# Linear attention with transposed outputs and divisors, and its jobs spread over steps of eight and six

## The chip, the core and the metric

The kernel runs on one NeuronCore of a Trainium2 chip, in one launch. The metric is the device time of that launch in microseconds (us). Five engines run beside each other, each through its own list of instructions in order: TensorE (PE in the profile; its weight loads have a row of their own, PEld), VectorE (DVE), ScalarE (ACT), GpSimd (POOL) and SyncE (SP, which issues most DMAs). They wait for each other through semaphores. Results of TensorE lie in PSUM, which the other engines read.

## The reference

Four transformer layers run one after the other on `x` (8 batches, 256 tokens, 256 features) with a context of the same shape, all in float32. The second layer, L1, is the one that changes. It has three linear attentions (one in an encoder layer on twice the context, two in a decoder layer on `x`) and two feed-forward blocks (256 to 512 to 256, ReLU), each followed by a layer norm that is added to the residual:

```python
def linear_attention(q, k, v):          # 8 heads of 32
    Q = jax.nn.elu(q) + 1.0
    K = jax.nn.elu(k) + 1.0
    vlen = v.shape[1]
    v = v / vlen
    KV = jnp.einsum('nshd,nshv->nhdv', K, v)
    Z = 1.0 / (jnp.einsum('nlhd,nhd->nlh', Q, K.sum(axis=1)) + EPS_ATTN)
    out = jnp.einsum('nlhd,nhdv,nlh->nlhv', Q, KV, Z) * vlen
    return out
```

The other layers: L0 and L3 have two softmax attentions and a feed-forward block each, L2 two softmax attentions and a mixture of eight experts with two chosen per token.

## The kernel before

All work is cut by batch, 8 units of 256 tokens. `Stream` (L736) holds the order of the work, written out by hand: every unit (`Item` for softmax attention, `Linear`, `Ffn`) puts its jobs at numbered steps, counted from the step at which the unit starts; `Stream.run` walks through the steps and emits the jobs of each, in the order in which they were put. A step has no length of its own: it lasts as long as its work. In an attention stage a step also holds one block of scores. The first stream holds L0, L1 and the attentions of L2; the experts and L3 follow.

L1 is the stretch of steps 160 to about 276. `e1` is the encoder's linear attention, `d0` and `d1` those of the decoder, `e2` and `d2` the feed-forward blocks. `e1`, `d0` and `e2` start a unit every 7 steps, so one of each lies in a period of 7. `d1` and `d2` start one every 4 steps; `d2` follows `d1` 14 steps behind. Before them `f0`, the feed-forward of L0, is still running; after them `sa2`, the self-attention of L2, starts with its projections beside the last `d2`.

The jobs of one `Linear` unit, with their step (L609):

- `turn` (0): TensorE transposes the input through PSUM, ACT copies it out (for `d1` the encoder's output too).
- `queries` (1): 4 matmuls into `ps_lq` (L524); `elu` (L506): DVE takes the minimum with 0 (L509), ACT the exponential (L510), and later DVE joins max(x, 0) with it (L514).
- `keys_values` (2): the joining for the queries, then 8 matmuls into one score tile, `s_kv` (L537), keys and values; the `elu` of the keys; ACT copies the values (`lv`, L544) beside a column of ones.
- `end_keys` (3): the joining for the keys; POOL adds a bias row to x.
- `sums` (4): keys times values (L555) into `ps_kv`; DVE masks the result to blocks of heads (L561) and builds four columns of key sums (L562), together `kv`, 132 wide.
- `mix` (6, twice): queries times `kv` (L569) for 128 tokens each; DVE adds the epsilon to the four divisors of a token, takes reciprocals of 8 numbers per partition (L574) and multiplies (L577).
- `turn_back` (8): TensorE transposes the result (L191), ACT copies it to `oT` (L584).
- `out` (9): 4 matmuls (L591), copied by ACT to `y` (L595). `norm_stats` (10), `norm` (11), `add` (13): the layer norm on DVE and POOL.

`Ffn` (L709) has `turn`, then `hidden` (L652, two of them in L1) and two outputs (L675) in the steps that follow, then its sum, norm and add.

PSUM pools: `ps_m` (2 buffers) for transposes, projections, `ps_kv`, hidden values and outputs; `ps_o` (2 buffers) for `lo` and for `ps_f`, the feed-forward's output; the two score tiles `sq` and `sk`, one each, which a unit of `Linear` uses by the parity of its batch. `y`, 4 buffers, holds the exponentials and the values under a norm.

A matmul of float32 is two records in the profile; an output of 256 columns by 256 inputs (4 matmuls) is "x8".

Of the kernel before, what the change touches and what calls it, by code (L numbers as in the profile page):

```python
# [90 lines left out]
def decoder_stack(ctx: ExitStack, tc: tile.TileContext, t: dict, out: bass.AP):  # L91
# [33 lines left out]
    def con(name):  # L125
        a, b = CONSTS[name]
        return cons[:, a:b]
# [6 lines left out]
    nc.gpsimd.memset(neg_half, -0.5)  # L134
    ones = const.tile([128, 128], F32, name="ones")
# [359 lines left out]
    class Linear:  # L495
# [10 lines left out]
        def elu(self, ps, name, bufs):  # L506

            e = work.tile([128, 2, 256], F32, tag="y", bufs=4, name="elu")
            nc.vector.tensor_scalar(e, ps, 0.0, None, ALU.min)  # L509
            nc.scalar.activation(e, e, AF.Exp)  # L510
            dst = stage_tile(name, bufs=bufs, name="l" + name)

            def rest():
                nc.vector.scalar_tensor_tensor(dst, ps, 0.0, e, ALU.max, ALU.add)  # L514
                return dst

            return rest

        def queries(self):
            w = self.sub["w"]  # L520
            ps = ps_m.tile([128, 2, 256], F32, tag="m", name="ps_lq")
            for i in range(2):
                for c in range(2):
                    nc.tensor.matmul(  # L524
                        ps[:, i, :], lhsT=w[:, c, i * 128 : (i + 1) * 128], rhs=self.xT[:, c, :], start=c == 0, stop=c == 1
                    )
            self.rest_q = self.elu(ps, "q0", 3)

        def keys_values(self):

            self.q = self.rest_q()
            w = self.sub["w"]
            s = scores["pool"].tile([128, 2, 2, 256], F32, tag="sq" if self.b % 2 else "sk", bufs=1, name="s_kv")
            for half in range(2):
                for n in range(2):
                    for c in range(2):
                        nc.tensor.matmul(  # L537
                            s[:, half, n, :], lhsT=self.kvT[:, c, n * 128 : (n + 1) * 128],
                            rhs=w[:, c, 256 + 256 * half : 512 + 256 * half], start=c == 0, stop=c == 1,
                        )  # L540
            self.rest_k = self.elu(s[:, 0], "q1", 3)
            self.v = stage_tile("k", (128, 2, 2, 129), 3, name="lv")
            nc.gpsimd.memset(self.v[:, :, :, 128:129], 1.0)
            nc.scalar.copy(self.v[:, :, :, 0:128], s[:, 1].rearrange("p n (i d) -> p n i d", i=2))  # L544

        def end_keys(self):
            self.k = self.rest_k()

            nc.gpsimd.tensor_tensor(self.x, self.x, over(self.sub["rows"][:, 1, :]), ALU.add)

        def sums(self):
            ps = ps_m.tile([128, 2, 256], F32, tag="m", name="ps_kv")
            for i in range(2):
# [6 lines left out]
            self.kv = kv = stage_tile("oq", (128, 2, 132), name="kv")  # L560
            nc.vector.tensor_tensor(kv[:, :, 0:128], ps[:, :, 0:128], over(con("blocks")), ALU.mult)  # L561
            nc.vector.tensor_tensor(  # L562
                kv[:, :, 128:132], ps[:, :, 128:129].to_broadcast([128, 2, 4]), over(con("heads")), ALU.mult
            )

        def mix(self, n):
            o = ps_o.tile([128, 2, 132], F32, tag="o", name="lo")
            for i in range(2):
                nc.tensor.matmul(  # L569
                    o[:, i, :], lhsT=self.q[:, i, n * 128 : (n + 1) * 128], rhs=self.kv[:, i, :], start=True, stop=True  # L570
                )
            z = small.tile([128, 2, 4, 1], F32, tag="z", name="z")
            nc.vector.tensor_scalar(z[:, :, :, 0], o[:, :, 128:132], 1e-6, None, ALU.add)
            nc.vector.reciprocal(z, z)  # L574
            if n == 0:
                self.o = stage_tile("yo", (128, 2, 256), name="lo_sb")
            nc.vector.tensor_tensor(  # L577
                self.o[:, n, :].rearrange("p (i h d) -> p i h d", i=2, d=32),
                o[:, :, 0:128].rearrange("p i (h d) -> p i h d", d=32), z.to_broadcast([128, 2, 4, 32]), ALU.mult,
            )  # L580

        def turn_back(self):
            self.oT = stage_tile("oT")
            transposed(self.o, lambda ps: nc.scalar.copy(self.oT, ps))  # L584
# [24 lines left out]
        def jobs(self, put):  # L609
            if self.sub.get("begin"):  # L610
                put(-3, self.sub["begin"], self.b)
            put(0, self.turn)
            put(1, self.queries)
            put(2, self.keys_values)
            put(3, self.end_keys)
            put(4, self.sums)
            put(6, self.mix, 0)
            put(6, self.mix, 1)
            put(8, self.turn_back)
            put(9, self.out)  # L620
            put(10, self.norm_stats)
            put(11, self.norm)
            put(13, self.add)

    class Ffn:
# [83 lines left out]
        def jobs(self, put):  # L709
# [3 lines left out]
            put(0, self.turn)  # L713
            n = self.f // 256
            for k in range(n):
                put(1 + k, self.hidden, k)
            if n == 4:
                for k in range(4):
                    put(n + 1 + k, self.out, k // 2, k % 2)
                end = n + 5  # L720
            else:
                for k in range(2):
                    put(n + 1 + k, self.out, k, 0)
                    put(n + 1 + k, self.out, k, 1)
                end = n + 3
# [10 lines left out]
    class Stream:  # L736
# [6 lines left out]
        def put(self, step, f, *args):  # L743
            self.at.setdefault(step, []).append(lambda: f(*args))

        def add(self, unit, start):
            unit.jobs(lambda step, f, *args: self.put(start + step, f, *args))
# [5 lines left out]
        def run(self):  # L753
            before = None
            for step in range(min(self.at), max([*self.at, *self.k]) + 2):
# [7 lines left out]
                for f in self.at.get(step, []):  # L763
                    f()
# [379 lines left out]
    def ffn(f, x, bias, hidden_bias=None, gain=None, post=False, last=False, end=None):  # L1144
        return {
            "f": f, "x": x, "bias": bias, "hidden_bias": hidden_bias, "gain": gain, "post": post, "last": last, "end": end,
        }
# [23 lines left out]
    f0 = ffn(DFF, own_x, 0, "L0_ffn", post=True)  # L1171
    e1 = {"x": the_enc, "kv": None, "begin": enc_first}
    e2 = ffn(2 * D, the_enc, 1, end=enc_store)
    d0 = {"x": own_x, "kv": None}
    d1 = {"x": own_x, "kv": the_enc, "begin": enc_load}
    d2 = ffn(2 * D, own_x, 1)
# [24 lines left out]
    follow(first, Linear, e1, 160, 7)  # L1201
    first.put(141, fill, d0, load_attn, "L1_d0", "L1_d0")
    follow(first, Linear, d0, 164, 7)
    follow(first, Ffn, e2, 174, 7)
    first.put(177, fill, d2, load_ffn, "L1_d", "L1_d2", 2 * D)
    first.put(220, fill, d1, load_attn, "L1_d1", "L1_d1")
    follow(first, Linear, d1, 225, 4)
    first.put(224, fill, sa2, load_attn, "L2_sa")
    follow(first, Ffn, d2, 239, 4)
    start = 239 + 11 + 14  # L1210
    attend(first, sa2, start)
    first.put(264, fill, ca2, load_attn, "L2_ca")
# [5 lines left out]
    f3 = ffn(DFF, own_x, 0, "L3_ffn", gain="L3_3", last=True)  # L1218
# [146 lines left out]
```

## Time and profile before

| | |
|---|---|
| time, median of 3 runs | 2501.59 us (2499.62 to 2510.47) |
| profiled execution | 2498.09 us, span 2496.3 us |
| mean granted TensorE clock | 0.955 |
| busy: PE / PEld / DVE / ACT / POOL | 2205.7 / 1654.2 / 1141.9 / 925.8 / 721.9 us |
| first `queries` of `e1` | 620.34 us |
| first `turn` of `d1` | 925.23 us |
| last `mix` of `d1` ends | about 1081.8 us |
| first step with both kinds of scores in `sa2` | 1129.42 us |

Times inside the span are counted from its start. The L1 stretch is the 509 us between the second and the last of these marks, a fifth of the span. A line of the timeline gives start and length in us, the engine, the line of the kernel, the operation, output and inputs, the count, and in brackets the idle time before it with what ended it. A line of the groups gives count, then busy us and mean ns of one, then idle time before them.

### The profile page before, as it was taken

The page shows a single profiled execution, that of the slowest core. Times are in us where ns is not written, and L with a number is a line of the kernel's source. Part 1 is how long each engine was busy: PE and PEld are TensorE (multiplying, and loading weights), DVE is VectorE, ACT ScalarE, POOL GpSimd, SP SyncE. Part 2 cuts the span into 40 slices and gives each one's busy share as a digit, 9 for nine tenths or more (in the row PEclk, how much of TensorE's full clock was granted, in tenths as well). Part 3 has the DMA queues.
Part 4 walks back from the last instruction along what each step waited for, and adds up shares of the span by engine and source line. Part 5 has one row for each costly group of instructions (what it writes and reads, how often), then busy time and mean ns, then how long its engine had stood idle before and what let it go on. Part 6 is the DMA issues. An engine that isn't in the chain of part 4 may idle for free.

```text
span 2496.3 us, 40268 instructions
## 1 busy us (share of the span) xinstructions
PE 2205.7 (88%) x17118; PEld 1654.2 (66%) x17118; DVE 1141.9 (46%) x2266; ACT 925.8 (37%) x1570; POOL 721.9 (29%) x781
## 2 busy tenths in 40 slices
PE   5888999999887788899999974799999599999899
PEld 4555666578776677776666543588888367766588
DVE  3545566733445454456777652100000355566521
ACT  1333355521222222235666531233332154555421
POOL 1011233333323231442334434222220533122131
PEclk8989999999999999999999987799999699999999
DMA  4170001000000020000000001355554100000000
GB/s 148 59 242 6 1 23 42 2 22 1 22 5 9 5 68 26 1 22 2 1 2 22 16 20 55 132 180 186 182 180 143 46 19 10 1 2 1 1 13 21
DMA packets 57059, 121.05 MB, mean 48 GB/s; under 512 B 6752, under 2 KB 40432, under 8 KB 50992
## 3 DMA queue, kind: packets, MB, share of 16 engines
q0 software_dynamic: 11904, 62.76, 7.1%
q1 hardware_dynamic: 44976, 55.73, 6.8%
q8 instruction: 134, 2.20, 0.4%
q14 instruction: 45, 0.37, 0.1%
HBM read 87.20 MB, written 31.20 MB: 47 GB/s over the span
## 4 chain that ended last, share of the span: by engine, by line
PE 79%; DVE 12%; POOL 2%; ACT 2%; issue 2%; DMA 2%; another core or an unknown queue 0%; SPq 0%; ACTq 0%; POOLq 0%; DVEq 0%
PE s_q L780 15%; PE ps_p L276 7%; PE s_e L1061 7%; PE ps_f L675 7%; PE ps_e L1070 6%; PE ps_h L652 6%; PE o L402 4%; DVE mx L372 4%; PE ps_v L329 4%; PE ps_out L426 4%; PE s_kv L537 3%; PE ps_t L191 3%; PE s_k L780 2%; PE s_q L776 2%; PE s_k L776 2%
## 5 line engine op out<-in xcount | busy, mean ns | idle before, releaser
L372 DVE TENSOR_REDUCE mx<-s_q 128x4 f32<-128x1024 f32 x320 | 392.3, 1226 | 355.9 <-PE s_k L780 310.1
L387 ACT ACTIVATE p<-s_k 128x1024 f32<-128x1024 f32 x320 | 327.8, 1024 | 411.9 <-PE s_k L780 401.0
L780 PE MATMUL s_q<-k,q 32*128 32x256 f32 (+1 forms) x3072 | 433.4, 400 | 28.5 <-DVE mx L372 28.4
L780 PE MATMUL s_k<-q,k 32*128 32x256 f32 (+1 forms) x3072 | 430.4, 398 | 8.8 <-ACT p L387 8.4
L780 PEld LDWEIGHTS s_q<-k,q 32*128 32x128 f32 x3072 | 258.2, 188 | 134.6 <-issue 53.7
L780 PEld LDWEIGHTS s_k<-q,k 32*128 32x128 f32 x3072 | 266.4, 187 | 19.9 <-ACT p L387 14.4
L204 POOL TENSOR_TENSOR rs<-ve,neg_half 128x2 f32<-128x2 f32 x120 | 87.0, 725 | 618.8 <-DVE ve L202 591.0
L414 POOL TENSOR_TENSOR yo<-oq,rec 128x256 f32<-128x256 f32 x96 | 60.0, 625 | 560.0 <-DVE rec L413 557.1
L402 PE MATMUL o<-p,va 128*32 128x256 f32 (+1 forms) x3072 | 201.7, 380 | 1.2 <-ACT p L387 1.2
L1061 PE MATMUL s_e<-eT,fc 128*128 128x256 f32 x736 | 170.7, 388 | 3.7 <-ACT eT L217 3.3
L1075 DVE COPY ye<-ps_e 128x512 f32<-128x512 f32 x23 | 15.9, 691 | 321.5 <-PE ps_e L1070 321.5
L1070 PE MATMUL ps_e<-fc,h 128*128 128x256 f32 x736 | 162.6, 379 | 0.0
L1061 PEld LDWEIGHTS s_e<-eT,fc 128*128 128x128 f32 x736 | 133.7, 192 | 34.4 <-ACT eT L217 6.8
L1070 PEld LDWEIGHTS ps_e<-fc,h 128*128 128x128 f32 x736 | 139.8, 190 | 19.0
L402 PEld LDWEIGHTS o<-p,va 128*32 128x32 f32 x3072 | 80.8, 110 | 94.4 <-issue 57.1
L1065 ACT ACTIVATE h<-s_e,fc 128x256 f32<-128x256 f32 x184 | 87.1, 474 | 143.4 <-PE s_e L1061 134.9
L652 PE MATMUL ps_h<-xT,w_L_w 128*128 128x256 f32 x512 | 121.8, 381 | 0.0
L776 PEld LDWEIGHTS <-ident_b 128*128 128x128 bf16 x1024 | 86.3, 102 | 53.0 <-issue 18.1
L675 PE MATMUL ps_f<-w_L_w,h 128*128 128x256 f32 x512 | 120.5, 379 | 0.0
L652 PEld LDWEIGHTS ps_h<-xT,w_L_w 128*128 128x128 f32 x512 | 96.6, 190 | 15.8 <-issue 2.3
L276 PE MATMUL ps_p<-qT,w_L_sa 128*128 128x256 f32 x384 | 102.5, 414 | 3.1 <-ACT qT L217 1.4
L311 ACT ACTIVATE k<-ps_p,cols,cons 128x256 f32<-128x256 f32 x192 | 97.6, 563 | 20.6 <-PE ps_p L276 14.6
(251 smaller groups left out, 3710.9 us busy)
## 6 DMA issues: line engine op xcount, KB each, us to landing
moe_rows<-zero SPq DMA_DIRECT2D x8, 2048.0 KB, 15.9
moe_results<-ye SPq DMA_DIRECT2D x23, 256.0 KB, 2.3
w_L_w<-in_L_w SPq DMA_DIRECT2D x4, 1024.0 KB
w_L_sa<-in_L_sa SPq DMA_DIRECT2D x3, 1024.0 KB, 5.0
w_L_ca<-in_L_ca SPq DMA_DIRECT2D x3, 1024.0 KB, 5.1
x_nat<-in_x SPq DMA_DIRECT2D x4, 512.0 KB, 6.7
mi<-in_mask_qk SPq DMA_DIRECT2D x8, 256.0 KB, 3.5
c_nat<-in_ctx SPq DMA_DIRECT2D x4, 512.0 KB, 9.8
```

The lines of the kernel that those rows point to most:

```text
L276: nc.tensor.matmul(ps, lhsT=self.w[:, c, at : at + 128], rhs=src[:, c, :], start=c == 0, stop=c == 1)
L329: nc.tensor.matmul(ps, lhsT=self.kv_in[:, c, n * 128 : (n + 1) * 128], rhs=self.w[:, c, 512:768], start=c == 0, stop=c == 1)
L372: nc.vector.tensor_reduce(out, s, AX.X, ALU.max, negate=True)
L387: nc.scalar.activation(p, s, AF.Exp, scale=DH**-0.5)
L402: nc.tensor.matmul(self.o[32 * j : 32 * j + 32, a, q0:], lhsT=self.va[:, kt, 8 * a + 2 * j + par, :], rhs=p[j // 2][:, j % 2, kt, q0:], st ...
L426: nc.tensor.matmul(self.po[:, n, :], lhsT=self.oT[:, a, n * 128 : (n + 1) * 128], rhs=self.w[:, a, 768:1024], start=a == 0, stop=a == 1,)
L652: nc.tensor.matmul(ps[:, i, :], lhsT=w1[:, c, at : at + 128], rhs=self.xT[:, c, :], start=c == 0, stop=c == 1)
L675: nc.tensor.matmul(self.po[:, n, :], lhsT=self.h[f // 4][:, f % 4, n * 128 : (n + 1) * 128], rhs=w2[:, f, :], start=f == 0, stop=f == nf - 1,)
L776: nc.tensor.matmul(o, lhsT=ident_b, rhs=m, start=half == 0, stop=False, skip_group_check=True)
L780: nc.tensor.matmul(o, lhsT=lhsT, rhs=rhs, start=half == 0 and not pen, stop=True, skip_group_check=True)
L1061: nc.tensor.matmul(s[:, i, :], lhsT=w1[:, c * DFF + f * 128 : c * DFF + f * 128 + 128], rhs=hT[:, c, :], start=c == 0, stop=c == 1,)
L1070: nc.tensor.matmul(po[:, n, :], lhsT=hs[f // 4][:, f % 4, n * 128 : n * 128 + 128], rhs=w2[:, f, :], start=f == 0, stop=f == 7,)
```

## The change

`Linear` computes its output already transposed: the second matrix is built with the key sums repeated over each head's block (`kv[:, 1]`, 128 wide) and the matrices become the stationary operands, so one `mix` gives, for all 256 tokens, the divisors (part 1) and the numerators (part 0) with features on partitions. `oT` is their quotient, which `out` takes as it is; `turn_back` is gone. The reciprocal is taken of the full tile, 512 numbers per partition. In `elu` the minimum is now a ReLU of -x on ACT. `queries` write to `ps_o`, `mix` to a score tile; each of `e1`, `d0`, `d1` has score tiles of its own.

`keys_values` is split into `keys` (step 2) and `values` (step 3), `out` comes at 6 instead of 9, and the jobs have ranks: within a step, rank 0 is emitted first, then 1 (the default), 2 and 3. `e1`, `d0` and `e2` now start a unit every 8 steps, `d1` and `d2` every 6; `d2` follows `d1` 11 steps behind and `sa2` starts at step 274 instead of 264. The steps of a feed-forward's jobs are given by hand. The loads of `d1` and `sa2` move by a few steps.

```diff
-        def elu(self, ps, name, bufs):
+        def elu(self, ps, name):
             e = work.tile([128, 2, 256], F32, tag="y", bufs=4, name="elu")
-            nc.vector.tensor_scalar(e, ps, 0.0, None, ALU.min)
-            nc.scalar.activation(e, e, AF.Exp)
+            nc.scalar.activation(e, ps, AF.Relu, scale=-1.0)
+            nc.scalar.activation(e, e, AF.Exp, scale=-1.0)
...
         def queries(self):
-            ps = ps_m.tile([128, 2, 256], F32, tag="m", name="ps_lq")
+            ps = ps_o.tile([128, 2, 256], F32, tag="o", name="ps_lq")
...
+        def end_queries(self):
             self.q = self.rest_q()
-            s = scores["pool"].tile([128, 2, 2, 256], F32, tag="sq" if self.b % 2 else "sk", bufs=1, name="s_kv")
...
+        def home(self, part):
+            return scores["pool"].tile([128, 2, 2, 256], F32, tag=self.sub["homes"][part], bufs=1, name="s_kv")
+        def keys(self):
+            self.s = self.home(0)
+            self.project(0)
+            self.rest_k = self.elu(self.s[:, 0], "q1")
+        def values(self):
+            self.project(1)
             self.v = stage_tile("k", (128, 2, 2, 129), 3, name="lv")
...
-            self.kv = kv = stage_tile("oq", (128, 2, 132), name="kv")
-            nc.vector.tensor_tensor(kv[:, :, 0:128], ps[:, :, 0:128], over(con("blocks")), ALU.mult)
-            nc.vector.tensor_tensor(
-                kv[:, :, 128:132], ps[:, :, 128:129].to_broadcast([128, 2, 4]), over(con("heads")), ALU.mult
-            )
+            self.kv = kv = stage_tile("oq", (128, 2, 2, 128), name="kv")
+            nc.vector.tensor_tensor(kv[:, 0], ps[:, :, 0:128], over(con("blocks")), ALU.mult)
+            nc.vector.tensor_tensor(kv[:, 1], ps[:, :, 128:129].to_broadcast([128, 2, 128]), over(con("blocks")), ALU.mult)
...
-        def mix(self, n):
...
-        def turn_back(self):
-            self.oT = stage_tile("oT")
-            transposed(self.o, lambda ps: nc.scalar.copy(self.oT, ps))
+        def mix(self):
+            self.s = self.home(1)
+            for part in (1, 0):
+                for i in range(2):
+                    nc.tensor.matmul(
+                        self.s[:, part, i, :], lhsT=self.kv[:, part, i, :], rhs=self.q[:, i, :], start=True, stop=True
+                    )
+            z = stage_tile("yo", name="z")
+            nc.scalar.activation(z, self.s[:, 1], AF.Identity, bias=eps_z)
             nc.vector.reciprocal(z, z)
+            self.oT = stage_tile("oT")
+            nc.vector.tensor_tensor(self.oT, self.s[:, 0], z, ALU.mult)
...
-            put(0, self.turn)
-            put(1, self.queries)
-            put(2, self.keys_values)
-            put(3, self.end_keys)
-            put(4, self.sums)
-            put(6, self.mix, 0)
-            put(6, self.mix, 1)
-            put(8, self.turn_back)
-            put(9, self.out)
-            put(10, self.norm_stats)
-            put(11, self.norm)
-            put(13, self.add)
+            put(0, self.turn, rank=2)
+            put(1, self.queries, rank=2)
+            put(2, self.end_queries, rank=0)
+            put(2, self.keys, rank=0)
+            put(3, self.values, rank=0)
+            put(4, self.sums, rank=0)
+            put(5, self.mix, rank=0)
+            put(6, self.out, rank=3)
+            put(7, self.norm_stats, rank=3)
+            put(8, self.norm, rank=3)
+            put(10, self.add)
...
-                for f in self.at.get(step, []):
+                for _, f in sorted(self.at.get(step, []), key=lambda job: job[0]):
                     f()
...
+    e1 = {"x": the_enc, "kv": None, "begin": enc_first, "homes": ("sq", "sq")}
+    d0 = {"x": own_x, "kv": None, "homes": ("sk", "sk")}
+    e2 = ffn(2 * D, the_enc, 1, (1, 2, 5, 6), end=enc_store)
+    d1 = {"x": own_x, "kv": the_enc, "begin": enc_load, "homes": ("sq", "sk")}
+    d2 = ffn(2 * D, own_x, 1, (2, 3, 4, 5))
...
-    follow(first, Linear, e1, 160, 7)
+    follow(first, Linear, e1, 160, 8)
-    follow(first, Linear, d0, 164, 7)
-    follow(first, Ffn, e2, 174, 7)
+    follow(first, Linear, d0, 164, 8)
+    follow(first, Ffn, e2, 174, 8)
-    follow(first, Linear, d1, 225, 4)
+    follow(first, Linear, d1, 225, 6)
-    follow(first, Ffn, d2, 239, 4)
-    start = 239 + 11 + 14
+    follow(first, Ffn, d2, 236, 6)
+    start = 274
     attend(first, sa2, start)
```

## The prediction

> **What bounds the kernel now.** I read the busy shares by stretch first, then TensorE's timeline, the waits on it, and the groups of DVE and ACT. The L1 stretch runs from the first `queries` of `e1` (620.34 us) to the first step with both kinds of scores (1129.42): 509.1 us. The stretches below are `e1`/`d0`/`e2`, `d1`/`d2`, and the way into `sa2`; the columns are length, then busy us of PE, PEld, DVE, ACT, POOL with counts, then the granted clock.
>
> ```profile
> 620.00:925.00 305.00, 246.16 (x1247) 211.58 (x1245) 153.01 (x409) 67.21 (x122) 92.20 (x101) 0.97 0.06 19
> 925.00:1082.00 157.00, 133.28 (x682) 113.91 (x683) 73.61 (x200) 44.79 (x80) 49.22 (x52) 0.97 0.06 17
> 1082.00:1129.00 47.00, 45.98 (x241) 35.63 (x240) 26.42 (x60) 13.96 (x28) 22.92 (x20) 1.00 0.09 29
> ```
>
> TensorE has most of the work in every stretch, but stands idle for 59 and 24 us in the first two. Where, the timeline of one period of 37.6 us shows (from one slow `ps_f` to the next):
>
> ```profile
> 732.31 3.54 PE L675 MATMUL ps_f<-w_L_e_w,h 128*128 128x256 f32 x8 [2.09 <-DVE z L573]
> ...
> 737.12 1.89 PE L675 MATMUL ps_f<-w_L_e_w,h 128*128 128x256 f32 x8
> 738.85 0.60 PE L191 MATMUL ps_t<-cons,lo_sb 128*128 128x128 f32 x4
> 739.29 1.89 PE L524 MATMUL ps_lq<-xT,w_L_d 128*128 128x256 f32 x8
> 741.02 0.61 PE L569 MATMUL lo<-kv,lq 128*128 128x132 f32 x4
> 743.16 0.72 PE L569 MATMUL lo<-kv,lq 128*128 128x132 f32 x4 [1.53 <-ACT y L690]
> ...
> 751.53 0.66 PE L191 MATMUL ps_t<-cons,lo_sb 128*128 128x128 f32 x4 [1.59 <-ACT xT L228]
> ...
> 756.99 1.97 PE L652 MATMUL ps_h<-xT,w_L_e_w 128*128 128x256 f32 x8 [2.09 <-DVE kv L562]
> 759.74 1.99 PE L591 MATMUL ps_out<-w_L_e,oT 128*128 128x256 f32 x8 [0.78 <-DVE h L660]
> ...
> 769.91 3.60 PE L675 MATMUL ps_f<-w_L_e_w,h 128*128 128x256 f32 x8 [2.09 <-DVE z L573]
> ```
>
> The idle times in brackets are 8.1 us of the period: short steps, in which a job of DVE or ACT has no matmul beside it. From start to start an x8 block takes 1.73 (737.12 to 738.85), a transpose group 0.44, one half of `mix` (x4) 0.45. The slow `ps_f` (3.60 for 1.89) is the clock:
>
> ```profile
> 769.90:773.40 3.50, 3.49 (x9) 2.79 (x10) 1.24 (x4) 0.00 (x0) 2.29 (x3) 0.52 0.00 0
> 951.00:954.50 3.50, 3.50 (x17) 3.05 (x16) 0.50 (x2) 1.13 (x2) 0.00 (x0) 0.52 0.67 212
> ```
>
> After an idle stretch of 2.09, and of 2.36 at 948.2, the granted clock is 0.52 for 3.5 us: 1.75 us lost. After idles of 1.5 to 1.6 it stays full.
>
> **The change, part by part.** TensorE per `Linear`: `turn_back` goes (0.44), `mix` grows from 4 x 0.225 = 0.90 to an x8 block of 1.73. That is +0.39, and 24 units make +9.4 us. An `e1`/`d0` unit becomes five blocks, one turn and `sums` (0.90): 9.97; `d1` has one turn more, 10.4; a feed-forward is 4 x 1.73 + 0.44 = 7.35.
>
> DVE and ACT are priced from these groups:
>
> ```profile
> L574 DVE RECIPROCAL z<-z 128x8 f32<-128x8 f32 x48 | 9.8, 203 | 1.7
> L413 DVE RECIPROCAL rec<-oq 128x16 f32<-128x16 f32 x96 | 24.3, 253 | 3.3
> L573 DVE TENSOR_SCALAR z<-lo 128x8 f32<-128x8 f32 x48 | 7.7, 159 | 9.6 <-PE lo L569 9.6
> L577 DVE TENSOR_TENSOR lo_sb<-lo,z 128x256 f32<-128x256 f32 x48 | 20.4, 424 | 1.7
> L514 DVE SCALAR_TENSOR_TENSOR lq<-s_kv,elu 128x512 f32<-128x512 f32 x24 | 16.5, 687 | 5.3 <-ACT lv L544 5.3
> L544 ACT COPY lv<-s_kv 128x512 f32<-128x512 f32 x24 | 13.6, 568 | 0.0
> L660 ACT ACTIVATE h<-ps_h 128x512 f32<-128x512 f32 x16 | 9.6, 599 | 23.9 <-PE ps_h L652 23.9
> ```
>
> The unknown price is a reciprocal of 512 numbers per partition. From 8 to 16 it grows by 50 ns, 6.25 ns each, where the plain operations L577 and L514 grow by 263 over 256 numbers, 1.03 each. On that line it is 203 + 504 x 6.25 = **3.35 us**. Bounds: 0.69, a plain operation of that size (L514), and 253 x 32 = 8.1, in proportion. I take the line, since both rows have hardly any spread.
>
> The Trainium skill, page "VectorE: DVE Perf Modes" (section "First, the fixed hardware budget"), gives the reciprocal a repeat count of 8, and a clock of 0.96 GHz in its specifications: 8.3 ns a number, an estimate of 4.4 us here. The two rows show 6.25; no row shows the large size. By the page the forecast below would be about 2492.
>
> So per unit DVE loses two minima (1.38), the epsilon and the reciprocal of 8 twice (0.72) and L577 twice (0.85), and gains 3.35, the quotient (0.69) and 0.27 for a `kv[:, 1]` of 256 numbers (0.42 for 0.15): +1.36. ACT loses a copy (0.59) and gains two ReLUs (0.60 each, L660) and the epsilon (0.57 + 0.10 for a bias by partition, as L665 at 0.47 stands to the copy L332 at 0.37): +1.28. The ReLU takes the minimum's place in the same chain (0.60 for 0.69). DVE goes from 18.3 to 21 us in an e period (91.7 busy in five), ACT from 8.3 to 10.9; the blocks of TensorE cover both, except in the place that follows.
>
> **The chain that is not covered.** In the built program ACT's epsilon waits for the last matmul of `mix`, not for its divisor half, and `out` waits for the quotient. From the start of the next block after `mix`, M: 0.20 until the result is seen (DVE saw `ps_lq` at 641.18, next block at 640.98), 0.67, 0.05, 3.35, 0.63, and 0.16 until TensorE starts: `out` at M + 5.06. On its engine all of TensorE queues behind `out`.
>
> *e period, 8 steps.* After `d0`'s `mix`: `queries` and `keys` of `e1`, 3.46, stall 1.60; then `out`, `values`, `ps_f`, `sums`, `ps_f`, turn, `mix` of `e1`, 9.98 and 0.1 to restart: 15.15. After it: `queries`, `keys`, turn, 3.89, stall 1.17; then `out`, `values`, hidden (5.2), `sums` (0.9), 0.77 until DVE has read the first hidden block behind a joining and a norm, hidden (1.8), 0.3 for `kv` behind the statistics, turn and `mix`: 16.4. Period **31.5**, against 37.6. No idle time exceeds 1.6, so no slow clock.
>
> *d period, 6 steps.* Between `mix` and `out` lie three turns, 1.3 us: stall 3.75, of it 2.6 in one piece (the last turn waits for a buffer until M + 2.0 and ends at 2.45). Then `out`, hidden, `queries`, `keys`, hidden, `values`, `ps_f`, `sums`, `ps_f`, `mix`: 16.5. Period **21.6**; now 21.25 with `d2` beside it (1039.17 to 1060.43) and 14.4 without. Here the slow clock comes back: 1.75 in, I take, four periods of five.
>
> Sum, from 620.34: to the second `mix` of `d0`, with `f0`'s rest as cover, 65.8; six e periods 189.0; to the third `mix` of `d1`, with the tail of `e2` beside it, 60.2; five d periods 108.0, plus 3.0 for `sa2`'s bias matmuls and 3.9 for its first projections; from the last `mix` to the first double scores 32.5 (8 score blocks of 1.07, six feed-forward blocks, `out`, projections, turns, a stall of 2.4; now 47.6, because three feed-forward units lie there and then two), and 2.0 for the last two `ps_f`, which fall among the double scores. That is 464.4 against 509.1: -44.7. The slow clock: 8 x 0.8 x 1.75 = +11. Together **-33.7**. The profiled execution took 2498.1, which becomes 2464; the median is 3.5 above it, so 2468.
>
> Everything before `f0`'s end and after `sa2`'s first steps has the same instructions in the same order. `d1`'s weights come three steps ahead (about 11 us; now 5.2 to land), the encoder's rows two steps (7 us; 4.5): hidden, and if not, 1 to 2 us once, at the first `d1`. SP passes no other transfer with them.
>
> **The rivals.**
>
> *Short reciprocal (0.69, the lower bound).* The chain is 2.4 us and under cover in the e periods: -2.8 x 6, -2.66 x 8 and no slow clock: 2419. The slope of the two rows is against it.
>
> *Long reciprocal (slower).* If a number costs more in a long operand, `out` waits that much longer 23 times (`e1`'s first unit has `f0`'s blocks beside it). At 4.8 us (9.1 ns a number) the 34 us are used up; at 8.1 it is +109: 2577. For it: nothing here is longer than 16. Against it: the line.
>
> *A reciprocal a third steeper.* At 8.3 ns a number, a third over the line and well below the proportional 15.8, it takes 4.4 us: 23 x 1.05 = +24, 2492. Of the rows, the smaller speaks for a slope no steeper than 6.5 (203 less 151 for a plain operation without its numbers, by 8). The page named above gives this price.
>
> *The stalls only move.* DVE takes its work in order, and a 3.35 us block stands before joinings, hidden values and `kv`. If these come late enough to keep the e period at 37.6, 36 us go: 2504. Against it: it is 67% busy there, and I found 0.77 + 0.3 us of such waits.
>
> **How the numbers follow.** Forecast 0.50, short 0.11, a third steeper 0.18, moved 0.11, long 0.10. No change within 0.5% means 2489 to 2514. Faster: the forecast, the short one and over half of the third (its time lies at the edge), 0.72; same: the rest of it and most of the moved, 0.15; slower: the long one and what is left, 0.13. The range 2430 to 2506 leaves out the long reciprocal and the far end of the short one.
>
> **What would show it.** Reciprocal groups of 3.3 us, 24 of them; e periods of 31.5 with stalls of 1.2 and 1.6 before `out`; d periods of 21.6 to 23.4 with a stall near 2.6 before `out` and a granted clock near 0.5 behind it. A reciprocal far from 3.35, or long idle times on TensorE before anything but `out`, would prove me wrong.

## The result, and the profile after

| | before | after |
|---|---|---|
| time, median of 4 runs each | 2506.03 us (2499.62 to 2511.68) | 2479.05 us (2476.01 to 2482.86) |
| ratio to before, 95% interval | | 0.9889 [0.9865, 0.9912] |
| profiled execution (its span) | 2498.09 (2496.3) us | 2481.54 (2479.8) us |
| busy: PE / DVE / ACT / POOL | 2205.7 / 1141.9 / 925.8 / 721.9 us | 2214.4 / 1172.6 / 959.0 / 714.5 us |
| L1 stretch | 509.1 us | 484.8 us (625.43 to 1110.25) |
| of it lost to the slow clock | 15.3 us | 10.2 us |
| L1 stretch without that loss | 493.8 us | 474.6 us |

The kernel is 1.1% faster. The loss to the slow clock is the sum of (1 - granted clock) over windows of about 4 us. It is taken out wherever stretches are compared, since it varies by 5 us and more from run to run of the same instructions: ahead of the stretch, where nothing was changed, the profiled executions lost 25.6 us before and 30.7 after. That is the 5.1 us by which the stretch starts later. The sum counts all time at the slow clock, also where TensorE stands idle and loses nothing; how much that can be is said with the experiments.

The same three parts of the stretch as in the prediction, now of the changed kernel (length, busy us of PE, PEld, DVE, ACT, POOL with counts, granted clock, DMA share, GB/s):

```profile
625.00:890.00 265.00, 231.27 (x1144) 196.83 (x1143) 165.22 (x296) 89.57 (x151) 86.95 (x97) 1.00 0.05 17
890.00:1075.00 185.00, 158.75 (x741) 133.90 (x742) 93.25 (x187) 58.76 (x103) 58.16 (x63) 0.94 0.07 22
1075.00:1110.00 35.00, 32.27 (x174) 23.74 (x173) 24.11 (x41) 11.78 (x24) 12.71 (x12) 1.00 0.11 38
```

Against before, the part of `e1`/`d0`/`e2` is shorter by 40 us, has 15 us less of TensorE's work and runs at full clock (0.97 before). The part of `d1`/`d2` is 28 us longer and runs at 0.94. The parts don't hold quite the same work, since units of `d1` begin at another place among the rest, so their sum is what counts.

An e period in TensorE's timeline (`mix` is L579, `out` is L593):

```profile
732.21 1.99 PE L593 MATMUL ps_out<-w_L_d,oT 128*128 128x256 f32 x8 [1.51 <-DVE oT L586]
...
740.55 1.89 PE L579 MATMUL s_kv<-lq,kv 128*128 128x256 f32 x8
...
747.41 1.99 PE L593 MATMUL ps_out<-w_L_e,oT 128*128 128x256 f32 x8 [1.07 <-DVE oT L586]
...
756.58 0.63 PE L193 MATMUL ps_t<-cons,enc 128*128 128x128 f32 x4 [0.81 <-DVE kv L572]
```

From `out` of `d0` at 732.21 to the next at 763.89 the period is 31.68 us, against 37.6 before. It has three idle times: 1.51 and 1.07 before the two `out`, and 0.81 before the turn ahead of a `mix`.

And a d period:

```profile
973.83 1.89 PE L579 MATMUL s_kv<-lq,kv 128*128 128x256 f32 x8
...
980.78 1.97 PE L593 MATMUL ps_out<-w_L_d,oT 128*128 128x256 f32 x8 [2.66 <-DVE oT L586]
...
995.56 1.89 PE L579 MATMUL s_kv<-lq,kv 128*128 128x256 f32 x8
```

It takes 21.73 us; where the clock is slow behind the stall (`out` at 957.36), 23.41.

The price that was unknown, in the groups, with ACT's step ahead of it:

```profile
L584 DVE RECIPROCAL z<-z 128x512 f32<-128x512 f32 x24 | 80.5, 3353 | 67.3 <-ACT z L583 67.3
```

The reciprocal of 512 numbers took 3.353 us, 24 times; the column behind it says that DVE always came to it from idling for ACT's epsilon (0.687 us by the same view). What TensorE then waited for, by releaser, from 625 to 1110 us (us in total, times, longest):

```profile
PE ps_out L593 <- DVE oT L586: 31.1, 20, 2.7
...
PE ps_t L193 <- DMA enc_in<-enc: 4.3, 1, 4.3
...
PE ps_lq L526 <- issue: 3.9, 1, 3.9
```

The first line is the stall that the prediction costed. The other two it had at nothing. The second stands before the first turn of `d1`, the third before the first `queries` of `d0`. "issue" names no releaser, so DVE's timeline must:

```profile
644.95 3.35 DVE L584 RECIPROCAL z<-z 128x512 f32<-128x512 f32 x1 [5.58 <-ACT z L583]
648.40 0.69 DVE L586 TENSOR_TENSOR oT<-s_kv,z 128x512 f32<-128x512 f32 x1
649.01 0.68 DVE L689 TENSOR_TENSOR y<-ps_f,x_nat 128x512 f32<-128x512 f32 x1
...
649.79 1.97 PE L526 MATMUL ps_lq<-xT,w_L_d 128*128 128x256 f32 x8 [3.88 <-issue]
```

`queries` (L526) write to `ps_o`. The buffer that they take is read last by the sum of `f0` (L689), and that sum stands in DVE's list behind `e1`'s first reciprocal: it ends at 649.69, and TensorE starts 0.10 later. The other wait begins on the sync queue (SPq):

```profile
885.54 0.33 SPq L163 DMA_DIRECT2D r_L_d<-in_rows  x1
885.97 0.37 SPq L1165 DMA_DIRECT2D enc_in<-enc  x1
...
SPq L163 <- POOL y L604: 8.9, 1, 8.9
...
889.92 0.81 PE L193 MATMUL ps_t<-cons,enc_in 128*128 128x128 f32 x4 [4.26 <-DMA enc_in<-enc]
890.52 3.44 PE L526 MATMUL ps_lq<-xT,w_L_d 128*128 128x256 f32 x8
```

`d1`'s weights were issued at 876.18. The bias rows next to them in the queue (L163) could not go before 885.54, since their buffer still served `e1`'s last norm; the third line, from the sync queue's own list of waits, names that norm's multiplication on GpSimd (L604), 8.9 us of waiting. The encoder's rows (L1165) were queued behind, and landed too late. The `queries` after the idle time took 3.44 us instead of 1.89, on the slow clock.

### The profile page after: what moved, and what is told of

Its sections match the earlier page's. It is cut to its first block, busy times and chain, and to the rows that moved or that the text cites. A ratio compares the mean times of both kernels' runs of the same rounds, so it can differ in the third digit from the quotient of the medians.

```text
span 2479.8 us, 40002 instructions
## 1 busy us (share of the span) xinstructions
PE 2214.4 (89%) x17022; PEld 1655.4 (67%) x17022; DVE 1172.6 (47%) x2122; ACT 959.0 (39%) x1618; POOL 714.5 (29%) x782
## 4 chain that ended last, share of the span: by engine, by line
PE 79%; DVE 13%; POOL 2%; ACT 2%; issue 2%; DMA 1%; another core or an unknown queue 0%; DVEq 0%; POOLq 0%; SPq 0%; ACTq 0%
PE s_q L781 15%; PE ps_p L278 7%; PE s_e L1062 7%; PE ps_f L676 6%; PE ps_e L1071 6%; PE ps_h L653 6%; PE o L404 5%; DVE mx L374 4%; PE ps_v L331 4%; PE ps_out L428 4%; DVE z L584 3%; PE ps_t L193 3%; PE s_k L781 3%; PE s_kv L542 2%; PE s_q L777 2%
## 5 line engine op out<-in xcount | busy, mean ns | idle before, releaser
L781 PE MATMUL s_k<-q,k 32*128 32x256 f32 (+1 forms) x3072 | 436.1, 402 | 8.5 <-ACT p L389 8.4
L777 PEld LDWEIGHTS <-ident_b 128*128 128x128 bf16 x1024 | 85.3, 100 | 54.0 <-issue 20.3
L584 DVE RECIPROCAL z<-z 128x512 f32<-128x512 f32 x24 | 80.5, 3353 | 67.3 <-ACT z L583 67.3
```

What stands on the lines that cost most here:

```text
L777: nc.tensor.matmul(o, lhsT=ident_b, rhs=m, start=half == 0, stop=False, skip_group_check=True)
L781: nc.tensor.matmul(o, lhsT=lhsT, rhs=rhs, start=half == 0 and not pen, stop=True, skip_group_check=True)
```

## The experiments

All are edits of the changed kernel. "Without clock" is the L1 stretch less its loss to the slow clock: 493.8 before, 474.6 after. Ratios are to the kernel before, timed on the same chip.

Behind a long idle time part of the slow clock falls on time in which TensorE has no work, and the loss taken out is then too large. Where the sum is weighted with TensorE's busy share, in windows of 0.5 us, the stretch without the clock is 494.4 before, 474.9 for the changed kernel, 489.8 and 479.2 for the two runs with `out` at 7, 461.5 for the same with its two edits, 472.4 for "rows later", 472.5 for "`queries` in the old bank" and 458.0 for "new order, old arithmetic"; the others move by 0.3 or less. Where it matters below, this second value is given too.

| run | stretch / clock loss / without clock, us | ratio, 95% interval |
|---|---|---|
| changed kernel again | 485.0 / 10.2 / 474.8 | 0.9895 [0.9859, 0.9932] |
| reciprocal left out | 442.0 / 3.4 / 438.6 | 0.9733 [0.9693, 0.9773] |
| `out` at 7, `add` at 11 | 513.1 / 32.4 / 480.7 | 1.0037 [1.0019, 1.0055] |
| `out` at 7, `add` at 10 | 494.3 / 20.5 / 473.8 | 0.9934 [0.9915, 0.9952] |
| the same, rows later, sum first | 475.7 / 17.1 / 458.6 | 0.9845 [0.9824, 0.9866] |
| rows later | 484.7 / 13.6 / 471.1 | 0.9906 [0.9873, 0.9939] |
| sum first | 480.6 / 10.2 / 470.3 | 0.9885 [0.9844, 0.9926] |
| `queries` in the old bank | 485.1 / 13.7 / 471.5 | 0.9897 [0.9859, 0.9934] |
| new order, old arithmetic | 467.0 / 10.2 / 456.8 | 0.9835 [0.9794, 0.9877] |
| old order, new arithmetic | 461.5 / 6.8 / 454.6 | 0.9812 [0.9772, 0.9851] |
| old order, new arithmetic, two waits mended | 457.3 / 3.4 / 453.9 | 0.9769 [0.9745, 0.9793] |
| new order, old arithmetic, three waits mended | 443.8 / 0.0 / 443.8 | 0.9734 [0.9716, 0.9752] |

### The changed kernel again

> The changed kernel again, unaltered, as the measure for the others of this group. Its L1 stretch (first queries of e1 to the first step with both kinds of scores) was 484.8 us; both theories expect 482 to 488, a ratio to the kernel before of 0.987 to 0.991.

485.0 us, and 474.8 without the clock, against 484.8 and 474.6: the stretch without its slow clock repeats to 0.2 us in this pair, so differences of a few us between runs can be read from it. The ratio, 0.9895, is that of the first comparison.

### What the reciprocal costs

```diff
-            nc.vector.reciprocal(z, z)
+            nc.vector.tensor_tensor(z, z, z, ALU.add)
```

> Leaves the reciprocal out: an addition of the same 512 numbers takes its place. Theory (out waits for the quotient, and the reciprocal's 3.35 us set that wait): the stalls of 1.51 and 1.07 before out vanish in each e period, so 31.7 becomes about 29; the 2.66 of the d period vanishes with its slow clock, so 21.7 to 23.4 becomes about 19.5; the wait of 3.9 beside f0 shrinks by 2.66. Stretch 484.8 - 19 - 24 - 3 = 439, ratio to before about 0.971. Rival (TensorE waits for DVE's whole list, 67% busy, not for this one operation): DVE loses 64 of its us but the other waits stay, stretch 465 to 475.

An addition takes the reciprocal's place, so this kernel doesn't compute the layer. 438.6 us without the clock. All 31.1 us of waits of `out` for `oT` are gone from the list of waits, and of the 3.9 before `d0`'s first `queries` 1.2 are left: together 33.8 of the 36.0 us of difference (474.6 - 438.6). The slow clock shrinks as well, from 10.2 to 3.4. So the length of this one DVE operation, not the matmuls or the copies added beside it, takes back 36 us of what the change gains.

### Later `out`, twice

The first run moves `out` and all that follows by a step:

```diff
-            put(6, self.out, rank=3)
-            put(7, self.norm_stats, rank=3)
-            put(8, self.norm, rank=3)
-            put(10, self.add)
+            put(7, self.out, rank=3)
+            put(8, self.norm_stats, rank=3)
+            put(9, self.norm, rank=3)
+            put(11, self.add)
```

> out, norm_stats, norm and add come one step later; nothing else. Theory (only the place of out decides, since the blocks of the next step cover the chain): two more blocks lie between mix and out, so the stalls of 1.51 and 1.07 vanish, and the 2.66 of the d period shrinks to under 0.5, with no slow clock there; stretch 484.8 - 18 - 24 = 443, ratio about 0.972. Rival (DVE's list is the bound; a later out only hands the wait on to the norm, the add and the next unit's turn): stretch 475 to 490, with new idle times before turns.

The theory failed: 480.7 (489.8 by the busy share), and no faster than before. The waits for `oT` did go, but DVE's and TensorE's timelines show a longer one in their place:

```profile
933.51 3.35 DVE L584 RECIPROCAL z<-z 128x512 f32<-128x512 f32 x1 [3.42 <-ACT z L583]
...
937.57 0.68 DVE L607 TENSOR_TENSOR x_nat<-y,x_nat 128x512 f32<-128x512 f32 x1
938.40 1.58 PE L193 MATMUL ps_t<-cons,x_nat 128*128 128x128 f32 x8 [3.92 <-DVE x_nat L607]
```

At step 11 of a unit, `add` (L607) stands on DVE behind the reciprocal of the unit six steps later, which is at its step 5 with rank 0. `d2`'s turn needs that sum. The d period went from 21.73 to 25.42 us (938.40 to 963.82), with a slow clock behind most of these idle times; the e period fell to 30.9 where the clock stayed full. The second run leaves `add` where it was:

```diff
-            put(11, self.add)
+            put(10, self.add)
```

> The changed kernel with out at step 7, norm_stats at 8, norm at 9, and add left at step 10, so that add doesn't stand behind the next unit's reciprocal on VectorE. Theory: the run with out at step 7 and add at step 11 lost its gain to add alone, which waited 3.35 us behind a reciprocal and held the second decoder's turn. With add at step 10 the stalls before out go (31 us in all in the changed kernel) and no wait for x_nat comes; the d periods fall from 21.7 to about 19.5 to 20, the e periods from 31.7 to about 30.9; the wait for the encoder rows of the first d1 unit (about 12 us in the earlier run) stays. The stretch without its slow clock: about 452 us against 474.6. Rival: VectorE's list as a whole sets the period, wherever out stands; then the stall only moves to another instruction, and the stretch stays at 470 us or more.

473.8 (479.2 by the busy share): the total is the rival's, and each theory holds in one half. In the d part the periods are 18.93 us (967.19 to 986.12), below what was expected, and no wait for `x_nat` is left. In the e part the period is 36.1 (720.81 to 756.95), longer than the 31.7 of the changed kernel, by this wait:

```profile
748.50 1.70 DVE L212 TENSOR_SCALAR y<-y,mv,rs 128x256 f32<-128x256 f32 x2 [0.22 <-POOL rs L206]
750.13 0.68 DVE L661 TENSOR_SCALAR h<-ps_h 128x512 f32<-128x512 f32 x1
...
750.95 2.06 PE L565 MATMUL ps_kv<-lv,lq 128*128 128x129 f32 x8 [3.47 <-DVE h L661]
```

The hidden block of `e2` was done on TensorE at 745.8. DVE, in a reciprocal from 738.65 to 742.0, came to the sum of `add` at 744.89, after 0.85 us of idling for the norm's multiplication on GpSimd, which now stands only one step ahead of it; behind that stood a norm's statistics, the keys and the norm's last step (L212); it read the hidden block (L661) at 750.13. `sums` waited for the buffer, and 2.06 us for 1.13 is the slow clock behind the idle time. So in the e part DVE's list, in its order, is what decides, as the rival says; `out` alone at another step only moves the place of the wait. It isn't that DVE has too much to do: it stands idle for 4.51 us ahead of its next reciprocal (759.60). `add` at 11 in the e part and 10 in the d part was not tried.

### Two waits that the prediction had at nothing

```diff
-    first.put(223, fill, d1, load_attn, "L1_d1", "L1_d1")
+    first.put(223, lambda: d1.update(w=load_w("wa", "L1_d1", 2, 1024)))
+    first.put(226, lambda: d1.update(rows=load_rows("L1_d1")))
```

> The bias rows of d1 are loaded three steps later than its weights instead of right behind them. Theory (SP held the first load of the encoder's rows back, because the rows before it waited for a buffer until e1's last norm): the 4.26 us before the first turn of the encoder's rows and the half clock behind it go, stretch 479, ratio to before 0.002 lower than the changed kernel's. Rival (the weights, 1 MB on the same queue, hold the transfer back): the load is issued earlier but lands no sooner, stretch 483 to 485.

The wait for `enc_in` is gone. In its place stand 0.38 us before the `queries` and a stall of 1.81 before the `out` that follows, which the 4.26 us had hidden; without the clock the stretch is 3.5 us shorter (471.1; 2.5 by the busy share). That the bias rows held the queue is shown. The time doesn't show the gain: the stretch with its slow clock is 484.7, not the 479 of the theory, since this execution lost 13.6 us to the clock for 10.2, 3.4 of it behind the wait before `d0`'s first `queries`, which in the first execution of the changed kernel brought no slow clock.

```diff
-            put(end, self.sum)
+            put(end, self.sum, rank=-1)
```

> The feed-forward's sum goes ahead of all else in its step (rank -1); nothing else. Theory (DVE takes f0's sum behind the first reciprocal, and d0's first queries wait for the ps_o buffer it frees): the wait of 3.9 goes, stretch without the reduced clock 470.7. Rival (the wait is for weights or for xT): 474 to 475.

The 3.9 us before `d0`'s first `queries` are gone; 470.3 without the clock, 4.3 less. Both edits are within the noise of the ratio, and are read from the stretch without its slow clock alone. Both were then put into the kernel with `out` at 7 and `add` at 10:

> The run above (out 7, norm_stats 8, norm 9, add 10) with d1's bias rows loaded three slots after its weights, behind the encoder loads on the sync queue, and with the sum of Ffn at rank -1, ahead of the reciprocal. Theory: the three waits have separate causes and add up: against the run above, the wait for the encoder rows (4 to 12 us) and the 3.9 us before the first decoder's queries go as well; the stretch without its slow clock about 438 to 442 us. Rival: the waits hide one another, and it gains under 5 us on the run above.

458.6, which is 15.2 less than without them (17.8 by the busy share). There the wait for `enc_in` was 11.9 us and fell to 1.7, and the 3.9 went: 14.1 in all. The waits add up, as the theory says; the level is higher than the 438 to 442 expected, since the e part of that kernel had not become what was expected of it (20.3 us of waits of `sums` for the hidden block), and since TensorE waited 7.0 us once for GpSimd's part of `sa2`'s bias (L492; 0.43 in the changed kernel). Why that came so late there was not looked into.

### `queries` in their old bank

```diff
-            ps = ps_o.tile([128, 2, 256], F32, tag="o", name="ps_lq")
+            ps = ps_m.tile([128, 2, 256], F32, tag="m", name="ps_lq")
```

> queries write to ps_m again, as before. Theory (the 3.9 us before d0's first queries are a wait for a ps_o buffer, which f0's sum frees only behind the reciprocal): that wait goes, but out of e1 then waits for the joining of d0's queries behind the quotient, 0.6 more in each e period; stretch without the reduced clock 474.6 - 3.9 + 4 = 475, a draw. Rival (banks of their own are worth much): 485 or more. If the wait of 3.9 stays, its cause is another.

471.5 without the clock, 3.1 less (2.4 by the busy share), and a ratio that can't be told from the changed kernel's. The 3.9 us wait went here too, since `queries` no longer share a bank with `f0`'s sums. The stall before `out` has kept its size and changed its name in part: 23.6 us for `oT` and 9.7 for `xT`, 33.3 together against 31.1. So the new bank for `queries` gives nothing in this order of steps.

### Half of the change at a time

The arithmetic of before (`kv` with 132 columns, divisors by row, `mix` in two halves, `turn_back`) in the new order:

```diff
-            put(5, self.mix, rank=0)
+            put(5, self.mix, 0, rank=0)
+            put(5, self.mix, 1, rank=0)
+            put(6, self.turn_back, rank=0)
```

> The new steps, ranks and projections with the old end of the unit: kv 132 wide, mix in two halves with reciprocals of 8 numbers, turn_back at step 6 ahead of keys, out at 6 as in the changed kernel. Times of the L1 stretch below are without what the reduced clock takes (before 493.8, changed kernel 474.6). Theory (the schedule brings the gain, the transposed output takes part of it back through its 5.1 us chain): e period 27 to 29 instead of 31.7, d period about 20 instead of 21.7, stretch 430 to 445, ratio to before 0.970 to 0.977. Rival (the transposed output brings the gain, as the waits of turn_back and its copy are gone): these waits come back, stretch 475 to 495.

And the new arithmetic in the order of before:

```diff
-            put(5, self.mix, rank=0)
-            put(6, self.out, rank=3)
+            put(6, self.mix)
+            put(9, self.out)
...
-    follow(first, Linear, e1, 160, 8)
+    follow(first, Linear, e1, 160, 7)
...
-    follow(first, Linear, d1, 225, 6)
+    follow(first, Linear, d1, 225, 4)
```

> The new arithmetic and projections in the old order: steps of seven and four, out three steps behind mix, no ranks in Linear. Theory (the reciprocal's chain costs only where too few blocks lie between mix and out): three steps cover it, no stall before out; the short steps of the old order keep 3 to 6 us of idle time in an e period; stretch without the reduced clock 455 to 475. Rival (the even spread and the ranks are what brought the gain): 485 to 500, as before.

Without the clock, the new order with the old arithmetic takes 37.0 us off the 493.8 of before, the new arithmetic in the old order 39.2, and both together 19.2. Either kernel with one half left out gains twice what the full change does. So the new arithmetic costs 17.8 us where it is put into the new order, and the new order 20.0 where it is put under the new arithmetic.

What each half is worth by itself is not shown. Both kernels keep the rest of the change: the ReLU on ACT, `queries` in `ps_o`, score tiles of their own for each attention, keys and values as two jobs. This rest was not run with the old order and the old arithmetic, and 37.0 and 39.2 both include what it gives, which may be much of them.

Why the halves don't go together, the waits say. In the new order with the old arithmetic the largest is

```profile
PE ps_out L601 <- ACT oT L594: 9.7, 7, 1.4
```

which is 9.7 us where the changed kernel has 31.1, since the old chain from `mix` to `oT` has no operation of 3.35 us. In the old order with the new arithmetic, where the reciprocal is 3.353 us as well, the largest is

```profile
PE ps_kv L565 <- POOL lv L555: 13.3, 11, 3.2
```

and only 1.5 us go to `out` for `oT`. There `out` is emitted three steps behind `mix`, and its start lies 10 to 15 us behind that of `mix`, so that the chain of 5.1 us is covered in all units but one. The new order puts `out` one step behind `mix`, with 3.5 to 3.9 us of blocks between them in the e part and 1.3 in the d part, three turns. The new arithmetic needs the distance that the new order takes away, and the new order the short chain that the new arithmetic takes away.

### Each half, mended

The old order with the new arithmetic, the memset of `lv`'s ones column moved from `values` to `queries`, and the sum of `Ffn` first:

```diff
         def queries(self):
+            self.v = stage_tile("k", (128, 2, 2, 129), 3, name="lv")
+            nc.gpsimd.memset(self.v[:, :, :, 128:129], 1.0)
...
-            self.v = stage_tile("k", (128, 2, 2, 129), 3, name="lv")
-            nc.gpsimd.memset(self.v[:, :, :, 128:129], 1.0)
...
-            put(end, self.sum)
+            put(end, self.sum, rank=-1)
```

> The new arithmetic in the old order (steps 7 and 4 apart, mix at 6, out at 9), with the memset of the ones column of lv moved from values to queries, two steps earlier on GpSimd, and the sum of Ffn at rank -1. Theory: the 13.3 us that TensorE waited for that memset in the run without the first edit (11 times, 3.2 us longest) were GpSimd's queue alone, and go; the stretch without its slow clock falls from 454.6 to about 443 us, the ratio to about 0.976. Rival: the memset only took the place of a wait for values or keys that ends at the same time; then 450 us or more.

453.9, as the rival says: the wait for GpSimd is gone, and the same `sums` now wait for the keys on DVE.

```profile
PE ps_kv L565 <- DVE lq L516: 12.7, 11, 2.5
```

Both came at the same time, and the e period is 29.93 us where it was 29.92. The ratio, 0.9769 against 0.9812, has an interval that overlaps with the earlier one, and shows no more than the stretch does.

The new order with the old arithmetic, `queries` in the old bank, and the two edits of the rows and the sum:

> The old arithmetic (a plain kv of 132 columns, divisors by row, turn_back at step 6) in the new order of steps, as in the earlier run, with the queries' sums in their old bank, d1's bias rows three slots later, and the sum of Ffn at rank -1. Theory: the wait for encoder rows (5.6 us) and the waits for lo's bank and for the queries' bank (3.9 and 5.6) go, those for oT (9.7) and y (5.9) stay: the stretch without its slow clock about 445 us against 456.8. Rival: the queries in the old bank wait there for the mix of the step before, and it stays within 4 us of 456.8.

443.8, as the theory says (445). Of the waits that it named, these two are left, with the numbers of the earlier run:

```profile
PE ps_out L601 <- ACT oT L594: 9.7, 7, 1.4
PE lo L579 <- ACT y L701: 5.9, 12, 0.7
```

No idle time in this stretch is followed by a slow clock (loss 0.0). The time is 2443.06 us (2442.15 to 2448.70), 2.7% below before, where the changed kernel is 1.1% below: it beats both kernels, and it doesn't use the transposed output.

## Why the prediction came out as it did

The forecast of 2468 from 2501.6 is a ratio of 0.9866; measured was 0.9889 [0.9865, 0.9912], so the sign was right, and so was the mechanism: the chain through the reciprocal, its stalls and the periods. The ratio forecast lies just inside the interval. The gain was put too high, by 6 us in the time (-33.6 forecast, -27.8 by the ratio) and by 9 in the stretch (-33.7 and -24.3).

- **The reciprocal.** Forecast 3.35 us from the line through 8 and 16 numbers, measured 3.353. The rivals with a short, a steeper and a long reciprocal all fall with it, and with them the estimate of 4.4 us from the Trainium skill's page "VectorE: DVE Perf Modes" (section "First, the fixed hardware budget"): 6.25 ns a number held to 512. That the reciprocal is what makes the stalls is shown by the run without it.
- **The chain from `mix` to `out`.** Forecast 5.06 us from the next block's start; in the d part 952.15 to 957.36 is 5.21. Its stalls were forecast at 1.60, 1.17 and about 2.6, measured 1.51, 1.07 and 2.66.
- **The periods.** Forecast 31.5 and 21.6, or 23.4 with the slow clock; measured 31.68, 21.73 and 23.41. The waits inside the e period were given as 0.77 + 0.3, and came as about 0.2 + 0.81.
- **The slow clock.** Forecast 11 us of loss, all in the d part, and none in the e part; measured 10.2 and 0.0. That the totals meet is in part luck. The forecast has a slow clock behind four in five of eight stalls; only four stalls of 2.66 us came, and three of them with a slow clock, 6.8 us of loss together, as one of the three lasted twice as long. The rest was lost behind the wait for `enc_in` (1.7) and behind 1.56 us of idle time before the `out` at 933.95 (1.7), a length after which the prediction expects the full clock. In the second execution of the same kernel the e part had a loss too, 1.7 us behind the 3.88 before `d0`'s first `queries` (654.81). The length of an idle time alone doesn't decide; the last section says what does.
- **The step that failed** is the edges of the sum, where idle time on TensorE before something other than `out` was named as what would prove it wrong. Without the clock the stretch was 474.6 for 464.4, and the pieces in the prediction's order are: to the second `mix` of `d0` 70.0 for 65.8; six e periods 189.7 for 189.0; to the third `mix` of `d1` 63.7 for 60.2; the five d periods with `sa2`'s blocks 116.7 for 114.9; the end 34.6 for 34.5. The first piece's error is the 3.88 us before `d0`'s first `queries`: the text took `f0`'s rest as cover for `e1`'s first reciprocal, and didn't ask what of that rest is itself queued behind the reciprocal on DVE, nor which bank the `queries`, moved to `ps_o`, would wait for. The third piece's is the sentence "SP passes no other transfer with them": it looked at what the moved loads are issued past, and not at the load beside them that waits for a buffer and holds the queue. It gave "1 to 2 us once" for a wait of 4.26 and the slow clock behind it. Both were shown by taking the cause away. In the fourth piece 1.74 us are a wait of `sa2`'s second projection for ACT's copy of its `q` (L300), which was not looked for.
- **The stalls only move**, the rival for 2504, didn't come about in the changed kernel: its e period is 31.68. It is what happened in the kernel with `out` at 7 and `add` at 10, whose e period is 36.1, by a mechanism of that kind: a hidden block that DVE comes to late.
- **What the prediction didn't see**, though its numbers hold it, is that the change works against itself. It costed the arithmetic and the order together, and so came near the sum without the finding that the kernel gains twice as much with either of them left out.

## What to carry to other kernels

A new long operation is paid for by what stands between its producer and its consumer, so a change that makes a chain longer and another that moves its two ends closer must be costed one at a time as well as together. Where an operation of several us is put on an engine that works in order, list what is queued behind it and who waits for that, in the first and last units above all, where other stages' work is in the same list. A load that waits for a buffer holds all loads issued behind it on its queue: when loads are moved, look at the ones beside them. And where two runs each leave out one half of a change, ask what else they both keep: they show what the halves do to each other, and not what each is worth.

## What the runs showed of the hardware

- The reciprocal on DVE grows in a straight line from 8 to 512 numbers per partition: 203, 253 and 3353 ns for 8, 16 and 512, so (3353 - 203) / 504 = 6.25 ns each, six times the 1.03 ns of the plain operations.
- The same idle time doesn't always bring the slow clock. Of the idle times of 2.65 to 2.66 us before `out` in the d part, those that ended at 957.36, 1002.51 and 1027.49 were followed by a block of 2.64 to 3.75 us, and the one that ended at 980.78 by one of 1.97. The Trainium skill's page "TensorE: Matmul & The Clock Gate" (section "What's actually happening") says that the clock is set by windows of about 3.4 us that run on whatever the kernel does. The traces agree. Read in windows of 3.413 us counted on from 890.24, the granted clock of the changed kernel is 0.50 or 1.00 in each of 720 windows, with nothing between; the slow ones of this stretch begin at 890.24, 934.61, 958.51, 1002.88 and 1026.77 (two in a row). What matters is how long TensorE idles within the window ahead: 2.27, 2.66 and 2.75 us ahead of the three slow blocks, where a border (978.99) cuts the idle times ahead of 980.78 into 1.74 in one window and 1.79 in the next. In the L1 stretch of the two kernels up to 1.79 us in a window never brought the slow clock, 2.08 or more always did, and between them it came once in six times (1.80, ahead of 934.61). The 3.88 us before `d0`'s first `queries` were cut into 1.98 and 1.90 and passed; in the second execution of the same kernel 3.28 of them fell into one window, and the clock was slow. So a time can change by 1.7 us without any change of the kernel. The page's advice to avoid idle times of over about 3 us (the Trainium skill, section "Why this matters for your kernels") is too mild here: 2.09 us in one window was enough five times in the kernel before.
- An addition of 128x512 on DVE, 0.68 us as a rule, took 1.41 us at 745.77 in the mended kernel with the old order, where GpSimd ran an addition of the same size from 745.37 on (1.26 us), and 1.51 us at 760.66, beside GpSimd's of 760.59 (1.03 us). At 753.21, with GpSimd idle, it took 0.68. No run was made to separate this, so it stands as an observation.
